# Larger sine slots, one exponential block for eight heads, and permuted rotary partners in an audio tower kernel

## The chip, the cores and the metric

The kernel runs on one core of a Trainium2 chip. A core has a matmul engine (PE in the profile), a vector engine (DVE), an activation engine (ACT), a general engine (POOL) and a queue engine that starts transfers (SP). Each works through its own list of instructions in order; semaphores hold an instruction until what it needs is there. The metric is the device time of one launch in microseconds (us).

## The reference

There are 32 sequences of audio. Each is cut into S = 313 frames of 512 samples, transformed (a cosine transform), and run through one layer: attention, then a feed-forward part in which every element goes through sines and cosines.

```python
h = einsum(frames, D)                              # 313 x 512 per sequence
h = h + attn(layernorm(h))                         # 8 heads of 64
h = h + ffn(layernorm(h))

# attention
Q = xpos(X @ W_Q, False); K = xpos(X @ W_K, True)  # x * cos + rot(x) * sin
p = softmax(Q @ K.T) * Dmat                        # decay gamma ** |n - m|
Y = groupnorm(p @ V)                               # over each head's 64
out = silu(X @ W_G) * Y @ W_O

# feed-forward, N = 256 units, D = 512 features
theta = x[..., None, :] / (1 + abs(W)) + B         # S x 256 x 512
idx = mod(round(theta * 4096 / (2 pi)), 4096)
cos_sum = sum(cos_tab[idx] * attn_cos, -1)         # over the 512 features
sin_sum = sum(sin_tab[idx] * attn_sin, -1)
out = silu(cos_sum @ proj_cos.T + sin_sum @ proj_sin.T)
```

The feed-forward part sets the size of the work: 32 x 313 x 256 x 512 angles, each with a sine and a cosine. With features on the 128 partitions that is 20.5 million elements per partition on ACT.

## The kernel before

**Feed-forward.** The 512 features are four chunks of 128 partitions (`c`), the 256 units are eight blocks of 32 (`UNITS`). Sequences are handled in pairs; pair p enters in round `STARTS[p]` and stays eight rounds, one for each block of units. So a round (`ffn_round`) works on one block for all pairs that are in: one to four pairs, that is r = 2, 4, 6 or 8 sequences. There are 42 rounds: 6 with r = 2, 8 with r = 4, 6 with r = 6 and 22 with r = 8. A *part* is one unit and one chunk for all r sequences. A *slot* takes as many parts as fit `SLOT` = 16 sequence-parts: 16 // r of them. In each slot

- DVE writes one index tile per part (`index`, L619), a second tile shifted by a quarter turn (`quarter`, L631), and wraps both (`mask`, L636), in int16;
- ACT takes two sines of the slot's tile (`sines`, L644: `trig<-ix`), one after the other, k = 1 and k = 0;
- PE sums over the features (`go`, L666): for each sequence and part a matmul with a 32 column weight (`hot`) that adds into row n of a PSUM bank (`pa`). Each is recorded as two instructions.

`ix` has three buffers of two halves, `trig` three, `hot` three. A `trig` buffer is free again when the matmuls of its slot have read it. The input `xT` of each pair stays in SBUF as long as the pair is in (`load_xT`, one load for each chunk). When a block is done DVE copies the bank (`part`, L684) and SP stores it in `sums_d`. After its eighth round, `output` loads the sums of a sequence (L531), projects them (four rows of `in_proj` through the two ring buffers), applies silu and adds the residual.

**Attention.** `attention` does one sequence: transform, layer norm, transposes, V, then for two halves of four heads: two times `columns` for q and k and, with weights whose neighbouring columns are swapped (`wq_s`, `wk_s`), for their rotary partners; multiplication by a table (`turn_qk`, L345) and addition (L349); for each head scores on PE (L359), the row maximum (L367) and a subtraction (L376) on DVE, but for each half's last head the maximum goes into ACT's bias. Then one ACT block `exps` per half: with `eng == "DVE"` one exponential over three heads (L383) and three over the last (L388), and a tiny Silu at the end (L396) that brings back the function table which the sines use. Then, head by head, transposes (L424), the decay (L436, from a tile `dec` loaded for each head) and the product with V (L442). Five sequences (the first two and three in the rounds with one pair) run with `eng == "ACT"`: there ACT does the evacuations and the exponentials of each head, with the row sums by accumulation; for the other 27 DVE does the sums.

**Order.** The kernel first collects all operations in a `Plan`: each has a key (its place in the intended order), an engine, an assumed duration and what it reads and writes. `emit` then plays them through: whichever engine is free next takes, of its operations that are ready, the one with the lowest key. The result is a fixed list for each engine. The first two sequences (buffers `A` and `B`) run before any sine and side by side; then `swap` gives B's space to the feed-forward part, and attention for the other 30 sequences, with buffers `A`, is spread over the rounds of sines so that each pair is ready in time.

Of the kernel before, what the change touches and what calls it, by code (L numbers as in the profile page):

```python
# [12 lines left out]
F32 = mybir.dt.float32  # L13
I32 = mybir.dt.int32
I16 = mybir.dt.int16
# [15 lines left out]
SLOT = 16  # L31
# [14 lines left out]
class Plan:  # L46
# [3 lines left out]
    WAIT = 400.0  # L50
    LAND = 3500.0
# [75 lines left out]
def tile_audio_tower(ctx: ExitStack, tc: tile.TileContext, t: dict, out: bass.AP):  # L127
# [6 lines left out]
    NB = 4  # L134
    N_RING = 2
    N_IX, N_TRIG, N_HOT, N_PA = 3, 3, 3, 4
# [10 lines left out]
    sums_d = dram.tile([2, P, 2, n_seq * S], F32, name="sums_d")  # L147
# [4 lines left out]
    class Buffers:  # L152


        def __init__(self, name, pool, psum):
# [3 lines left out]
            self.probs = [(name, "prob", a) for a in range(NB - 1)]  # L159
# [5 lines left out]
            self.dec = sb("dec", STEP * (NT - 1) + S)  # L165

            self.u = sb("u", NC4, S)
            self.qk = [self.u[:, 2 * i : 2 * i + 2, :] for i in range(2)]
# [3 lines left out]
            self.prob = sb("prob", NB - 1, NT, S)  # L172
            self.probT = sb("probT", NT, S)

            self.exp = [*(self.prob[:, a] for a in range(NB - 1)), self.probT]
            wide = self.prob.rearrange("p a b s -> p (a b s)")
            self.wide = wide
            self.turn = wide[:, NT * S : NT * S + 4 * S].rearrange("p (i s) -> p i s", s=S)
# [118 lines left out]
    def attention(plan, keys, sq, x, eng):  # L297
# [20 lines left out]
        hs, probs, us = x.rows_of, x.probs, x.every("u", 2)  # L318
# [14 lines left out]

        for hb in range(H // NB):
            for g in range(hb * NB // 2, (hb + 1) * NB // 2):
                key = step(4)
                qk = x.qk[g % 2]
                kq = x.k("u", g % 2)
                columns(plan, key, x, 0, t["wq"][g])
                columns(plan, key, x, 1, t["wk"][g])  # L340

                columns(plan, key, x, 2, t["wq_s"][g])
                columns(plan, key, x, 3, t["wk_s"][g])
                plan.add(key, "DVE", 1500,
                         lambda: nc.vector.tensor_tensor(  # L345
                             x.turn, x.W[:, :, :S], turn_qk, ALU.mult),
                         x.banks(0, 1, 2, 3), probs[1:])
                plan.add(key, "DVE", 870,
                         lambda qk=qk: nc.vector.tensor_tensor(  # L349
                             qk, x.turn[:, 0:2], x.turn[:, 2:4], ALU.add),  # L350
                         probs[1:], (kq,))
            for hd in range(hb * NB, (hb + 1) * NB):
                key = step(2.5)
                a, r0 = hd % NB, (hd % 2) * DH
                qk, kq = x.qk[hd // 2 % 2], x.k("u", hd // 2 % 2)
                for i in range(NT):
                    plan.add(
                        key, "PE", 660,
                        lambda i=i, qk=qk, r0=r0: nc.tensor.matmul(  # L359
                            x.W[:N, i, :S], qk[r0 : r0 + DH, 0, ROW0[i] : ROW0[i] + N],  # L360
                            qk[r0 : r0 + DH, 1, :], start=True, stop=True,
                        ),
                        (kq,), x.banks(i),
                    )
                m = x.mx[hd % 2]
                plan.add(key, "DVE", 1150,
                         lambda m=m: nc.vector.tensor_reduce(m[:N], x.W[:N, :NT, :S], AX.X, ALU.max),  # L367
                         x.banks(0, 1, 2), (x.k("mx", hd % 2),))
                if a == NB - 1:

                    plan.add(key, "DVE", 100,
                             lambda m=m: nc.vector.tensor_scalar(m[:N], m[:N], -1.0, None, ALU.mult),
                             (), (x.k("mx", hd % 2),))
                    continue
                plan.add(key, "DVE", 1150,
                         lambda m=m, a=a: nc.vector.tensor_tensor(  # L376
                             x.prob[:N, a], x.W[:N, :NT, :S],
                             m[:N].unsqueeze(2).to_broadcast((N, NT, S)), ALU.subtract),
                         (x.k("mx", hd % 2), *x.banks(0, 1, 2)), (probs[a],))

            def exps(hb=hb, m=m):
                if eng == "DVE":
                    nc.scalar.activation(x.prob[:N], x.prob[:N], AF.Exp)  # L383
                for a in range(NB):
                    for i in range(NT):
                        last = a == NB - 1
                        if last or eng == "ACT":
                            nc.scalar.activation(  # L388
                                x.exp[a][:N, i, :],
                                x.W[:N, i, :S] if last else x.exp[a][:N, i, :], AF.Exp,  # L390
                                bias=m[:N, i : i + 1] if last else 0.0,
                                accum_out=x.sm[:N, i, hb * NB + a : hb * NB + a + 1]
                                if eng == "ACT" else None,
                            )

                nc.scalar.activation(x.lu[:1, 0:1], x.lu[:1, 0:1], AF.Silu)  # L396
            plan.add(step(), "ACT", 10500 if eng == "ACT" else 6700, exps,
                     (x.k("mx", 1), *x.banks(0, 1, 2)),
                     [*probs, x.k("probT"), x.k("sm", hb), x.k("lu")])
            if eng == "DVE":  # L400
                h0 = hb * NB
                plan.add(step(0), "DVE", 1190,
                         lambda h0=h0 + NB - 1: nc.vector.tensor_reduce(
                             x.sm[:N, :, h0], x.probT[:N], AX.X, ALU.add),
                         (x.k("probT"),), (x.k("sm", hb),))
                plan.add(step(0), "DVE", 3160,
                         lambda h0=h0: nc.vector.tensor_reduce(
                             x.sm[:N, :, h0 : h0 + NB - 1].rearrange("p i h -> p h i"),
                             x.prob[:N], AX.X, ALU.add),
                         probs, (x.k("sm", hb),))  # L410

            for hd in (hb * NB + a for a in (3, 2, 0, 1)):
                key = step(5)
                a = hd % NB
                ka = (*probs, x.k("probT"))[a]
                plan.add(key, "SP", DMA_NS,
                         lambda hd=hd: nc.sync.dma_start(x.dec, t["decay"][hd]),
                         (), (x.k("dec"),))
                for jj in range(NT):
                    j = NT - 1 - jj  # L420

                    def go(a=a, jj=jj, j=j):
                        for i in range(NT):
                            nc.tensor.transpose(  # L424
                                x.W[:N, jj, ROW0[i] : ROW0[i] + N],
                                x.exp[a][:N, i, ROW0[j] : ROW0[j] + N], ident[:N, :N],
                            )
                    plan.add(key, "PE", 800, go, (ka,), x.banks(jj))

                def decayed():  # L430
                    window = x.dec[:N].rearrange("p (a s) -> p a s", a=1)
                    w3 = bass.AP(
                        tensor=window.tensor, offset=window.offset,
                        ap=[list(window.ap[0]), [STEP, NT], [1, S]],
                    )
                    nc.vector.tensor_tensor(x.probT[:N], x.W[:N, :NT, :S], w3, ALU.mult)  # L436
                plan.add(key, "DVE", 1150, decayed, (x.k("dec"), *x.banks(0, 1, 2)),
                         (x.k("probT"),))
                for i in range(NT):
                    def go(i=i, hd=hd):  # L440
                        for jj in range(NT):
                            nc.tensor.matmul(  # L442
                                x.y[:N, i, (hd % 2) * DH : (hd % 2 + 1) * DH],
                                x.probT[:N, jj, ROW0[i] : ROW0[i] + N],
                                x.h[:N, jj, hd * DH : (hd + 1) * DH],
                                start=(jj == 0), stop=(jj == NT - 1),
                            )
                    plan.add(key, "PE", 1000, go, (x.k("probT"), hs[hd // 2]), x.banks(3))
                if a not in (2, 1):
                    continue  # L450


                h0 = hd // 2 * 2
                plan.add(
                    step(), "DVE", 560,
                    lambda h0=h0: nc.vector.tensor_copy(  # L456
# [121 lines left out]
    def ffn_round(plan, k0, blk, ring):  # L578
# [22 lines left out]
        for parts in slots:  # L601
            first, last = parts is slots[0], parts is slots[-1]
            E = len(parts) * r * S
            for n, c in dict.fromkeys((n // 2 * 2, c // 2 * 2) for n, c in parts):
                if (n, c) in hot:
                    continue
# [351 lines left out]
```

## Time and profile before

| | |
|---|---|
| median of 3 runs | 18688.12 us (18686.35 to 18691.65) |
| the profiled execution | 18689.4 us |
| its span, first to last instruction | 18687.6 us |
| ACT busy | 18069.0 us, 97% |
| DVE busy | 17425.4 us, 93% |
| PE busy | 14667.1 us, 78% |
| sines (L644) | 4288 instructions, 17529.0 us of ACT |
| first sine | 353.6 us after the start |
| transfers | 783.70 MB, 42 GB/s mean |

The profile lists instruction groups by source line, engine and operation; behind the bar stands the idle time of the engine just ahead of them and what ended most of it. A long mean of an ACT or DVE row can overlap with its neighbour, so busy time divided by the count, or a run of equal instructions in the timeline, gives the price of one more.

### The profile page before, as it was taken

To read this page: it belongs to the slowest core of one execution; us is meant where nothing else is said; L and a number is where in the kernel's file an instruction comes from. 1 tells how busy PE (TensorE), PEld (TensorE's weight loads), DVE (VectorE), ACT (ScalarE), POOL (GpSimd) and SP (SyncE) were. 2 spreads that over 40 slices of the span, in tenths; PEclk is the share of its full clock that TensorE was granted. 3 is DMA by queue.
4 is the path that set the end of the run, shared out by engine and by line. 5 is a ranking of instruction groups with operands and counts; after the bars stand their busy time and mean duration, and the time that the engine had idled before them with its cause. 6 is when DMAs were issued, how large, how long until landed. Compare 5 with 4: busy or idle time off the path is not lost. (4 is left out here: it accounts for less than half of the span.)

```text
span 18687.6 us, 332496 instructions
## 1 busy us (share of the span) xinstructions
PE 14667.1 (78%) x148864; PEld 6569.4 (35%) x148864; DVE 17425.4 (93%) x12972; ACT 18069.0 (97%) x5026; POOL 944.3 (5%) x1222
## 2 busy tenths in 40 slices
PE   8788888888787887888787888887888887766566
PEld 5443333333333333333333333333333333222222
DVE  5899999999999999999999999999999999889998
ACT  3899999999999999999999999999999999999998
POOL 0001000000000000000000000000000000000000
PEclk8899999999999999999999999999999999889988
DMA  3211111111111111111111111111111111000011
GB/s 93 62 55 47 53 58 47 49 52 49 31 34 38 47 41 42 34 37 49 38 46 40 32 45 41 46 42 41 34 38 49 39 46 37 21 10 25 13 31 48
DMA packets 716483, 783.70 MB, mean 42 GB/s; under 512 B 72336, under 2 KB 470928, under 8 KB 715056
## 3 DMA queue, kind: packets, MB, share of 16 engines
q1 hardware_dynamic: 715056, 762.43, 13.7%
q8 instruction: 1169, 19.15, 0.4%
q14 instruction: 258, 2.11, 0.0%
HBM read 657.51 MB, written 104.66 MB: 41 GB/s over the span
## 5 line engine op out<-in xcount | busy, mean ns | idle before, releaser
L644 ACT ACTIVATE trig<-ix 128x5008 f32<-128x5008 int16 (+1 forms) x4288 | 17529.0, 4176 | 274.4 <-PE pa L666 157.3
L666 PE MATMUL pa<-trig,hot 128*32 128x313 f32 x131072 | 10264.9, 458 | 3322.3 <-ACT trig L644 3268.9
L666 PEld LDWEIGHTS pa<-trig,hot 128*32 128x32 f32 x131072 | 4033.6, 115 | 9141.6 <-ACT trig L644 4999.8
L619 DVE TENSOR_SCALAR ix<-xT,f 128x2504 int16<-128x2504 f32 (+3 forms) x5888 | 6658.2, 1182 | 49.3 <-DMA xT<-xT_d 31.3
L636 DVE TENSOR_SCALAR ix<-ix 128x10016 int16<-128x10016 int16 (+1 forms) x2144 | 5687.0, 2653 | 67.5
L631 DVE TENSOR_SCALAR ix<-ix 128x5008 int16<-128x5008 int16 (+1 forms) x2144 | 3029.4, 1413 | 622.0 <-ACT trig L644 485.3
L292 PE MATMUL a_W<-a_xnT,a_ring 128*128 128x313 f32 x4960 | 1514.5, 444 | 73.5 <-DVE a_prob L345 32.0
L277 PE MATMUL a_W<-a_ring,a_u 128*105 128x512 f32 x2256 | 1098.8, 619 | 84.7 <-DMA a_u<-in_frames 30.3
L292 PEld LDWEIGHTS a_W<-a_xnT,a_ring 128*128 128x128 f32 x4960 | 888.3, 190 | 693.8 <-issue 301.0
L442 PE MATMUL a_W<-a_h,a_probT 105*105 105x64 f32 x4464 | 540.7, 271 | 72.4 <-DVE a_probT L436 71.4
L277 PEld LDWEIGHTS a_W<-a_ring,a_u 128*105 128x105 f32 x2256 | 356.9, 174 | 683.0 <-issue 616.1
L442 PEld LDWEIGHTS a_W<-a_h,a_probT 105*105 105x105 f32 x4464 | 478.8, 182 | 326.4 <-issue 204.2
L228 POOL TENSOR_TENSOR a_gu<-a_gr 105x24 f32<-105x24 f32 x93 | 86.4, 929 | 9806.9 <-DVE a_gr L222 9802.1
L359 PE MATMUL a_W<-a_u 64*105 64x313 f32 x1488 | 485.3, 454 | 93.2 <-DVE a_prob L376 67.0
L277 PE MATMUL a_W<-a_ring,a_xnT 128*105 128x512 f32 x744 | 367.8, 618 | 30.0 <-DVE a_xnT L214 28.8
L359 PEld LDWEIGHTS a_W<-a_u 64*105 64x105 f32 x1488 | 232.7, 172 | 355.4 <-DVE a_prob L376 131.0
L228 POOL TENSOR_TENSOR a_lu<-a_lr 105x3 f32<-105x3 f32 x186 | 145.4, 782 | 3833.3 <-DVE a_lr L222 3823.5
L264 PE MATMUL a_W<-ident,a_h 105*128 105x105 f32 x1116 | 182.8, 293 | 158.0 <-DVE a_h L252 77.1
L367 DVE TENSOR_REDUCE a_mx<-a_W 105x3 f32<-105x939 f32 x248 | 279.8, 1128 | 20.0 <-PE a_W L359 19.8
L436 DVE TENSOR_TENSOR a_probT<-a_W,a_dec 105x939 f32<-105x939 f32 x248 | 279.7, 1128 | 19.3 <-PE a_W L424 17.1
L424 PE MATMUL a_W<-ident,a_prob 105*105 105x105 f32 x1674 | 243.2, 276 | 15.8 <-DVE a_h L456 15.8
L345 DVE TENSOR_TENSOR a_prob<-a_W,turn_qk 128x1252 f32<-128x1252 f32 x124 | 180.4, 1455 | 73.5 <-PE a_W L292 37.3
(138 smaller groups left out, 3748.7 us busy)
## 6 DMA issues: line engine op xcount, KB each, us to landing
hot<-in_hot SPq DMA_DIRECT2D x1344, 128.0 KB
a_dec<-in_decay SPq DMA_DIRECT2D x248, 260.5 KB
a_ring<-in_proj SPq DMA_DIRECT2D x128, 256.0 KB
a_ring<-in_dct SPq DMA_DIRECT2D x124, 256.0 KB
a_ring<-wv_d SPq DMA_DIRECT2D x124, 256.0 KB
a_ring<-in_wq SPq DMA_DIRECT2D x124, 256.0 KB
a_ring<-in_wk SPq DMA_DIRECT2D x124, 256.0 KB
a_ring<-in_wq_s SPq DMA_DIRECT2D x124, 256.0 KB
```

The lines of the kernel that those rows point to most:

```text
L277: lambda c=c, i=i, k=k, to=to: nc.tensor.matmul(x.W[:N, to, :], lhsT[:, c, ROW0[i] : ROW0[i] + N], x.ring[k], start=(c == 0), stop=(c == N ...
L292: lambda c=c: nc.tensor.matmul(x.W[:, bank, :S], w[:, c, :], x.xnT[:, c, :], start=(c == 0), stop=(c == NC4 - 1)),
L359: lambda i=i, qk=qk, r0=r0: nc.tensor.matmul(x.W[:N, i, :S], qk[r0 : r0 + DH, 0, ROW0[i] : ROW0[i] + N], qk[r0 : r0 + DH, 1, :], start=Tru ...
L367: lambda m=m: nc.vector.tensor_reduce(m[:N], x.W[:N, :NT, :S], AX.X, ALU.max),
L424: nc.tensor.transpose(x.W[:N, jj, ROW0[i] : ROW0[i] + N], x.exp[a][:N, i, ROW0[j] : ROW0[j] + N], ident[:N, :N],)
L436: nc.vector.tensor_tensor(x.probT[:N], x.W[:N, :NT, :S], w3, ALU.mult)
L442: nc.tensor.matmul(x.y[:N, i, (hd % 2) * DH : (hd % 2 + 1) * DH], x.probT[:N, jj, ROW0[i] : ROW0[i] + N], x.h[:N, jj, hd * DH : (hd + 1) * ...
L619: nc.vector.tensor_scalar(now["ix", x][:, 0, d0 : d0 + 2 * m * S], now["xT", c][:, 2 * at * S : 2 * (at + m) * S], f[:, 0, c, n : n + 1], ...
L631: nc.vector.tensor_scalar(tl[:, 1, :E], tl[:, 0, :E], float(LUT // 4), None, ALU.add)
L636: nc.vector.tensor_scalar(tl, tl, LUT - 1, LUT // 2, ALU.bitwise_and, ALU.bitwise_xor)
L644: nc.scalar.activation(tl[:, :E], now["ix", x][:, 1 - k, :E], AF.Sin, bias=-PI32, scale=ANG)
L666: nc.tensor.matmul(now["pa", p][g * 32 : g * 32 + 32, :S], now["hot", hot[n - u, c // 2 * 2]][:, u, c % 2, k, :], now["trig", w][:, s0 : s ...
```

## The change

Several edits come together.

1. `SLOT` goes from 16 to 24 sequence-parts. The `ix` buffers become five single halves in one tile, taken two at a time in turn, so that every fifth slot has halves that don't lie side by side and is wrapped by two `mask` instructions. `trig` goes from three buffers of 16 to two of 24, `hot` from three to four of the same bytes. Parts go chunk by chunk (all 32 units of a chunk, then the next), and `xT` and the scales `f` are loaded for each chunk of each round into two buffers, for all r sequences at once, so that one `index` instruction does a part.
2. `exps` stands once for all eight heads. `prob` grows from three heads to eight; every head subtracts its maximum on DVE; the decay writes back into `prob`; the decay tiles lie in the two halves of `u`; the table `turn_qk` is loaded for each sequence into `prob`'s space.
3. For the first two sequences `wq_s` and `wk_s` are not used: ACT copies q and k to SBUF, and a matmul with a permutation `swap_m` makes their partners.
4. `affine` and `centre` (one-time preparation of weights) get keys that place them after the start of the first sequences; `affine` no longer writes `h`.
5. `sums_d` is laid out by block: four sequences are stored by one transfer, and `output` loads eight pieces per sequence where it loaded two.
6. The scheduler's constants: `WAIT` 400 to 300, `LAND` 3500 to 2500, 150 ns for 169 per matmul of `go`.

```diff
-SLOT = 16
+SLOT = 24
...
-    WAIT = 400.0
-    LAND = 3500.0
+    WAIT = 300.0
+    LAND = 2500.0
...
-    N_IX, N_TRIG, N_HOT, N_PA = 3, 3, 3, 4
+    N_X, N_IX, N_TRIG, N_HOT, N_PA = 2, 5, 2, 4, 4
...
+            if swap_m is None:
                 columns(plan, key, x, 2, t["wq_s"][g])
                 columns(plan, key, x, 3, t["wk_s"][g])
+            else:
+                copy(plan, key, eng, 2 * S, x.raw, x.W[:, 0:2, :S], x.banks(0, 1), probs[-1:])
+                for i in range(2):
+                    plan.add(key, "PE", 550,
+                             lambda i=i: nc.tensor.matmul(x.W[:, 2 + i, :S], swap_m, x.raw[:, i, :],
+                                                          start=True, stop=True),
+                             probs[-1:], x.banks(2 + i))
...
+        def exps():
+            if eng == "DVE":
+                for a in range(0, H, 4):
+                    nc.scalar.activation(x.prob[:N, a : a + 4], x.prob[:N, a : a + 4], AF.Exp)
+            else:
+                for a in range(H):
                     for i in range(NT):
+                        nc.scalar.activation(x.prob[:N, a, i, :], x.prob[:N, a, i, :], AF.Exp,
+                                             accum_out=x.sm[:N, i, a : a + 1])
+
+            nc.scalar.activation(x.lu[:1, 0:1], x.lu[:1, 0:1], AF.Silu)
+        plan.add(step(2), "ACT", 18200 if eng == "ACT" else 9500, exps,
+                 (), [*probs, x.k("sm"), x.k("lu")])
+        if eng == "DVE":
+            for a in range(0, H, 2):
+                plan.add(step(0), "DVE", 2080,
+                         lambda a=a: nc.vector.tensor_reduce(
+                             x.sm[:N, :, a : a + 2].rearrange("p i h -> p h i"),
+                             x.prob[:N, a : a + 2], AX.X, ALU.add),
+                         probs[a : a + 2], (x.k("sm"),))
...
-        todo = [(n + u, c) for n in range(0, UNITS, 2) for c in range(NC4) for u in range(2)]
+        todo = [(n, c) for c in range(NC4) for n in range(UNITS)]
...
+            for c in dict.fromkeys(c for n, c in parts):
+                if c not in xs:
+                    y, fz = xs[c], fs[c] = place("xT", N_X), place("f", N_X)
...
+                    plan.add(key - 10, "SP", DMA_NS,
+                             lambda c=c, y=y: nc.sync.dma_start(
+                                 new("xT", y, [P, RING * S], bufs=N_X)[:, : r * S],
+                                 xT_d[:, c, sq0 * S : (sq0 + r) * S]),
+                             [("xT_d", sq0 + b) for b in range(r)], (("xT", y),))
...
-            x = place("ix", N_IX)
+            x = [place("ix", N_IX) for _ in range(2)]
...
+                for i in ([slice(x[0], x[1] + 1)] if x[0] < x[1] else [slice(i, i + 1) for i in x]):
+                    nc.vector.tensor_scalar(ix[:, i, :E], ix[:, i, :E], LUT - 1, LUT // 2,
+                                            ALU.bitwise_and, ALU.bitwise_xor)
...
-    affine(plan, -2000.0, A)
+    affine(plan, -999.9, A)
...
-    centre(plan, -1999.0, B)
+    centre(plan, -999.93, B)
```

## The prediction

> **What bounds the kernel now.** I read the engines' shares first, then the busy time by stretch of the span, then ACT's groups by shape and ACT's waits.
>
> ```profile
> PE 14667.1 (78%) x148864; PEld 6569.4 (35%) x148864; DVE 17425.4 (93%) x12972; ACT 18069.0 (97%) x5026; POOL 944.3 (5%) x1222
> ```
>
> ACT is busy for all but 618.6 us of the span. The stretches say where those lie (columns: length, busy PE, weight loads, DVE, ACT, POOL, clock, DMA share, GB/s):
>
> ```profile
> 200.00:300.00 100.00, 92.33 (x385) 68.03 (x384) 46.07 (x56) 22.64 (x58) 7.32 (x26) 0.71 0.22 66
> ...
> 400.00:1000.00 600.00, 484.97 (x4286) 252.50 (x4278) 541.50 (x664) 494.31 (x222) 34.46 (x52) 0.89 0.21 62
> ...
> 5000.00:15000.00 10000.00, 8080.53 (x82744) 3594.39 (x82748) 9502.80 (x6123) 9995.33 (x2559) 554.13 (x684) 0.95 0.14 41
> ```
>
> There are three regimes. Until the first sine (353.6 us) PE carries the first two sequences. From there to about 1000 us ACT, DVE and PE are all near full and wait for each other. From 5000 to 15000 us ACT has no gap (99.95%), while DVE has 5% and PE 19%. So after the ramp an ACT microsecond saved is a microsecond of time, as long as nothing new makes ACT wait. What ACT is made of:
>
> ```profile
> L644 ACT ACTIVATE trig<-ix 128x5008 f32<-128x5008 int16 x3520 | 15046.3, 4363 | 218.2 <-PE pa L666 138.6 <-DVE ix L636 53.6 <-DVE a_u L349 13.7
> L644 ACT ACTIVATE trig<-ix 128x3756 f32<-128x3756 int16 x768 | 2483.0, 3319 | 56.2 <-issue 19.2 <-PE pa L666 18.7 <-DVE ix L636 14.9
> L383 ACT ACTIVATE a_prob<-a_prob 105x2817 f32<-105x2817 f32 x54 | 138.0, 2555 | 0.6
> ...
> ACT trig L644 <- PE pa L666: 157.3, 78, 7.1
> ACT trig L644 <- DVE ix L636: 68.5, 46, 10.4
> ```
>
> The last two rows are waits (total, times, longest). By stretch, the 157.3 us for PE fall as 78 in 400 to 1000 us, 59 in 1000 to 4000, about 6 in 4000 to 16000 and 14 at the end.
>
> **What the Trainium skill says.** "ScalarE: Activation LUTs", section What ACT_TABLE_LOAD costs: one element per cycle at 0.833 ns, 186 ns for an instruction with immediate operands, of which back-to-back ones hide 93; a table load is 1283 ns, and a drain of about 1380 ns makes a switch about 2.66 us. The trace agrees on slope, overlap and the 1283 ns, but shows no drain: the next instruction begins within 0.02 us of the load's end. "Perfetto Trace Analysis", section Optimization Strategy: repeated gaps on an engine that should be full can mean too few buffers. That is the thing to fear of `trig` going from three to two.
>
> **The change, part by part.**
>
> *Sines.* Built, the changed program's order has 2688 sines of 7512 elements, 56 of 5008 and 16 of 2504: 2760 for 4288, with the same 20.5 million elements. So 1528 instructions' fixed time goes. Runs of equal sines price it:
>
> ```profile
> 8154.05 158.00 ACT L644 ACTIVATE trig<-ix 128x5008 f32<-128x5008 int16 x37
> ...
> 17298.24 503.06 ACT L644 ACTIVATE trig<-ix 128x3756 f32<-128x3756 int16 x156
> ```
>
> That is 4.270 and 3.225 us each, 0.835 ns per element and 88 ns fixed; with the skill's 0.833 ns the fixed part is 98. 1528 x 88 to 98 = 134 to 150; I take **-145**. All of it is on the bound.
>
> *Exponentials.* A half now takes 6.50 us of ACT from load to Silu (8147.55 to 8154.05 in the timeline): two loads of 1.28, 2.55, three of 0.44, 0.20. The new block is two loads, two instructions of 3756 (2.555 + 939 x 0.833 ns = 3.34 each, 0.1 overlapped) and 0.2: 9.28. 27 sequences x (13.00 - 9.28) = **-100**. Of the five ACT sequences, three run beside sines and save a pair of loads and a Silu, 2.8 each: **-8**. This rests on no Exp being left between sines, which the order shows.
>
> *Start.* For the first two sequences 64 matmuls of 128x313 go (2.28 us per four at the timeline's clock, 36 us) and 16 of that size come (9 us), PE being 92% busy there. The ACT copy between (626 elements; 1252 take 1.19 us, so some 0.65) is covered: three or four matmuls of the other sequence stand in PE's order between. Two more subtractions of 1.14 us for each sequence (5 us) lie on DVE, about full while scores run. Moving `affine` and `centre` behind the first loads lets PE start before 16.1 us, where it now waits for `in_dct` behind 2.7 MB of other loads; the same 14 us of DVE come later, beside PE's transform. But the first slot takes DVE 12.7 instead of 8.4 us. -27 + 5 - 4 + 4 = **-22** on the first sine's time; from -45 to +10, since one block of 48 exponentials for both sequences (0.45 each, 21 us) now stands where two shorter ones were, and PE may wait for B's.
>
> *Waits of ACT for PE.* Not shown by the trace, so bounded. A group of matmuls takes PE 2.31 us for 16 (a run of 32 instructions at full clock; 2.47 by busy time over count), so 3.5 to 3.7 for 24. With three buffers of 16 PE could be 6.0 us late before ACT stopped; with two of 24 it is 6.36 - 3.7 - 0.1 = 2.6 us. Attention's matmuls stand between the groups in PE's order. I charged each its time (0.58 to 0.62 us for 128x313, 0.88 to 0.97 for 512 columns, 0.20 to 0.24 for PV), took off what a period leaves free (2.65 us, now 1.8), carried the rest on, and called what exceeds the slack a wait. For the order before this gives 87 to 203 us, and 157 were measured; for the order after 155 to 356. The larger groups are 6 matmuls of 512 (5.3 us) and 8 of 313 (4.6 us) in one go, where PE used to take 2 or 3. Scaled: +50 in the ramp to 1000 us, +40 to 4000, +35 to 15000, -5 at the end, of which some falls into time in which DVE holds ACT anyway: **+100**, from 0 (attention stands still for transfers just where it would pile up) to +200.
>
> *DVE.* Index instructions fall from 5888 to 5376 (208 ns fixed, from 626 at 541 and 2504 at 1539 ns: -106), quarters by 764 (156 ns: -119), masks by 488 (173 ns: -84); 64 more subtractions at 1.136 (+73), 64 fewer sign changes (-11), row sums even. -247 in 17425: DVE keeps its distance to ACT. Five halves let it run 1 to 2 slots (13 to 25 us) ahead, where two slots were 17 us. I take **-20** off the 68.5 us, 0 at worst.
>
> *SP and transfers.* `xT` and `f` are 168 loads each for 64 and 42; `xT` adds 144 MB (8 GB/s on 42). They are keyed 10 half-slots (64 us) ahead and a buffer lasts a quarter of a round (35 us at r = 2, 136 at r = 8). The queue gets 4138 entries for 4049; the decay loads stop holding it (2180 us waiting for L436 with one buffer). The table load per sequence waits for heads 4 and 5 of the sequence before; only the first rotary step needs it. I cost these at nothing, hidden under running sines; if the cover is gone, each late chunk stalls DVE, then ACT. At the end one slot is shorter and six more small loads per sequence (0.6 us each) stand before the last projection: **+4**.
>
> Sum: -145 - 100 - 8 - 22 + 100 - 20 + 4 = -191 on the profiled 18689.4 (span 18687.6), giving 18498; the median is 1.3 us below that. I take 18490.
>
> **The rivals.**
> *The cover holds* (0.27): the late matmuls cost nothing new, ACT idles as before. -145 - 100 - 8 - 22 - 20 + 4: 18398. For it: the measured waits from 5000 to 15000 us are 1.6 us, where the count gave up to 27. Against: in the ramp the count comes out near the waits.
> *Two sine buffers make PE the pacemaker* (0.09): 722 of the groups have more than 2.65 us of attention ahead of them in PE's order. If each costs ACT 0.7 us, because attention also waits for DVE in mid-burst with the sine matmuls queued behind, it is 505 us on the 18398 of the case above: 18903. It is slower than before from 0.4 us per group (290 gained over 722). Against: it needs such waits in the middle stretch, where today there are none.
> *Late chunks* (0.10): 1 us for each of 168 chunk changes, PE's +100 on top: 18660. For: `xT` reloads are new in every round, up to 1.28 MB each. Against: the DMA share is 14%.
> That the change doesn't do what it says is excluded for the counts (they are in the built order); not for the start.
>
> **How the numbers follow.** The main case (0.48) is 18490, between 18400 and 18590 by the bounds of the start and of PE's waits. The rest, 0.06, is small mishaps around no change. About 0.2%, 37 us, is what a measurement of this kernel can tell from no change. Faster by more: main, cover and most of late chunks, 0.86; within: 0.05; slower: 0.09. Range 18350 to 18660.
>
> **What would show it.** After the change ACT's group of sines should be 2760 strong with about 17384 us; ACT busy about 17816, idle about 681; one pair of table loads per sequence; the first sine near 330 us. The row of sines waiting for PE should be about 250 us; near 157 is the second case, above 500 the third. DVE waiting for `xT` above 100 us is the fourth. I am wrong if ACT's busy time falls by much other than 255 us, or if its idle time leaves 550 to 750 us.

## The result, and the profile after

The kernel after takes 18588.61 us (median of five runs, 18575.13 to 18593.15), the kernel before 18688.12 us on the same chip (five runs, 18683.11 to 18698.63). The ratio is 0.9944, 95% interval 0.9931 to 0.9957: about 105 us less, from 80 to 129 (the medians differ by 99.5). The forecast was 18490 with a range of 18350 to 18660. The direction and the range held; the gain is about half of what was predicted. The profiled execution of the kernel after took 18593.15 us, with a span of 18591.2 us, 96.4 less than before.

The shares of the engines, as the page of the kernel after has them:

```profile
PE 14520.5 (78%) x148768; PEld 6791.6 (37%) x148768; DVE 17165.7 (92%) x11210; ACT 17827.2 (96%) x3248; POOL 968.9 (5%) x1222
```

ACT's busy time fell by 241.8 us (18069.0 to 17827.2), and DVE's by 259.7. But the span fell by only 96.4, so ACT's idle time rose by 145.4 (618.6 to 764.0). ACT's groups show the first half of this (first all sines, then groups by shape), and the rows of waits (who waits for whom: total, times, longest) show the second, with two rows of the kernel before at the end:

```profile
L636 ACT ACTIVATE trig<-ix 128x7512 f32<-128x7512 int16 (+1 forms) x2760 | 17398.1, 6386 | 456.8 <-PE pa L658 229.7
...
L636 ACT ACTIVATE trig<-ix 128x7512 f32<-128x7512 int16 x2688 | 17122.8, 6453 | 423.8 <-PE pa L658 200.9 <-DVE ix L628 128.1 <-issue 80.0
...
L400 ACT ACTIVATE a_prob<-a_prob 105x3756 f32<-105x3756 f32 x54 | 177.1, 3327 | 0.3
...
L407 ACT ACT_TABLE_LOAD x32 | 41.1, 1283 | 0.6
...
L400 ACT ACT_TABLE_LOAD x27 | 34.6, 1283 | 0.5
```

```profile
ACT trig L636 <- PE pa L658: 229.7, 132, 8.8
...
ACT trig L636 <- DVE ix L628: 128.1, 56, 13.4
...
ACT trig L636 <- issue: 81.3, 21, 7.4
...
PE a_W L282 <- DMA a_u<-in_frames: 52.9, 21, 6.5
```

```profile
ACT trig L644 <- issue: 27.9, 11, 5.8
...
PE a_W L277 <- DMA a_u<-in_frames: 30.3, 9, 7.2
```

There are 2760 sines in all with 17398.1 us, against 4288 with 17529.0. One pair of table loads is left for each of the 27 sequences with `eng == "DVE"`. The three waits of the sines, for PE, for DVE and for nothing the profile names ("issue"), were 157.3, 68.5 and 27.9 us before. They are now 72, 60 and 53 longer. One stretch of the span shows most plainly that something new is there (length, busy PE, weight loads, DVE, ACT, POOL, clock, DMA share, GB/s):

```profile
5000.00:15000.00 10000.00, 7971.06 (x82855) 3728.56 (x82857) 9439.75 (x5534) 9883.89 (x1657) 592.60 (x671) 0.93 0.16 50
```

From 5000 to 15000 us ACT had no gap before (9995.33 busy); now 116 us are missing there, though DVE (94%) and PE (80%) are both less loaded than before. So no engine has become too full on the average of this stretch; some work seems to come at the wrong moment.

The first sine now comes 316.2 us after the start (353.6 before):

```profile
316.18 25.53 ACT L636 ACTIVATE trig<-ix 128x7512 f32<-128x7512 int16 x4 [10.47 <-DVE ix L628]
```

The span can be made up from these numbers. ACT's busy time gives -241.8 us. Its idle time until the first sine fell from 300.7 to 264.8, that is -35.9. After the first sine it rose from 317.9 to 499.2, that is +181.3. Together this is -96.4.

**One case of an "issue" wait.** The timeline of the kernel after (start, length, engine, line, count, and in brackets the wait ahead of it), cut to PE, ACT and SP's queue:

```profile
9011.59 0.34 SPq L596 DMA_DIRECT2D xT<-xT_d  x1
9011.98 0.42 SPq L326 DMA_DIRECT2D a_u<-in_frames  x1
...
9018.60 5.71 PE L282 MATMUL a_W<-a_ring,a_u 128*105 128x512 f32 x8 [4.82 <-DMA a_u<-in_frames]
...
9024.24 3.37 PE L658 MATMUL pa<-trig,hot 128*32 128x313 f32 x48
...
9027.73 12.82 ACT L636 ACTIVATE trig<-ix 128x7512 f32<-128x7512 int16 x2 [4.66 <-issue]
```

The load of the frames (`in_frames`, 626 KB) goes out 0.4 us behind a chunk of `xT` of 1252 KB. PE has reached the transform of the next sequence (L282), stands for 4.8 us and starts 6.6 us after the load was issued. The sine group at 9024.24 is queued behind it, ends at 9027.6, and only then is a `trig` buffer free: the sine starts at 9027.73. The wait is called "issue", but what it goes back to is a transfer two steps earlier.

The place in the queue matters. From 6700 to 15300 us the kernel after issues 16 loads of frames, and the timeline shows PE waiting for 14 of them. Seven of the 14 were issued 0.4 us behind a chunk of `xT`, and PE started 6.5 to 7.2 us after their issue; it waited 30.5 us for these in all. The other seven had no chunk just ahead, and PE started 3.8 to 4.7 us after their issue; it waited 3.7 us for these.

**One case of a wait for PE**, from the timeline at 5123 us (PE and ACT, and one copy on DVE):

```profile
5123.41 5.40 PE L282 MATMUL a_W<-a_ring,a_xnT 128*105 128x512 f32 x12
5128.73 3.37 PE L658 MATMUL pa<-trig,hot 128*32 128x313 f32 x48
5132.03 5.40 PE L282 MATMUL a_W<-a_ring,a_xnT 128*105 128x512 f32 x12
...
5138.64 0.48 DVE L675 COPY part<-pa 128x313 f32<-128x313 f32 x1
...
5140.03 6.53 PE L658 MATMUL pa<-trig,hot 128*32 128x313 f32 x96 [2.60 <-ACT trig L636]
5143.51 12.82 ACT L636 ACTIVATE trig<-ix 128x7512 f32<-128x7512 int16 x2 [3.54 <-PE pa L658]
```

Two lumps of six matmuls with 512 columns (5.40 us each, two recorded instructions for one matmul) stand close together in PE's order, and ACT's next sine waits 3.54 us. Lumps of this kind are what the prediction counted, but here they explain only a part. PE is through with the second lump at 5137.43, yet its next sine group starts at 5140.03, and the profile puts these 2.60 us down to ACT. Had the group (3.37 us) started at once, the sine would have waited about 0.9 us by estimate. The stand falls at the turn of a round: by the code, this group is the first of the new round in two PSUM banks that the round before had filled, and DVE's last copy of them (`part`, L675) ran from 5138.64 to 5139.12. The kernel after also has one `part` buffer where the kernel before has two. Whether that is the cause, and what it is worth elsewhere, was not tested.

### The profile page after: what moved, and what is told of

Same layout as the page of the kernel before. It is cut to its first block, busy times and chain, and to the rows that moved or that the text cites. A ratio compares the mean times of both kernels' runs of the same rounds, so it can differ in the third digit from the quotient of the medians.

```text
span 18591.2 us, 325962 instructions
## 1 busy us (share of the span) xinstructions
PE 14520.5 (78%) x148768; PEld 6791.6 (37%) x148768; DVE 17165.7 (92%) x11210; ACT 17827.2 (96%) x3248; POOL 968.9 (5%) x1222
## 5 line engine op out<-in xcount | busy, mean ns | idle before, releaser
L636 ACT ACTIVATE trig<-ix 128x7512 f32<-128x7512 int16 (+1 forms) x2760 | 17398.1, 6386 | 456.8 <-PE pa L658 229.7
L658 PEld LDWEIGHTS pa<-trig,hot 128*32 128x32 f32 x131072 | 4291.2, 118 | 9312.4 <-ACT trig L636 4578.4
L612 DVE TENSOR_SCALAR ix<-xT,f 128x2504 int16<-128x2504 f32 (+3 forms) x5376 | 6499.2, 1268 | 431.6 <-ACT trig L636 389.4
L628 DVE TENSOR_SCALAR ix<-ix 128x15024 int16<-128x15024 int16 (+4 forms) x1656 | 5581.8, 3385 | 41.1
L621 DVE TENSOR_SCALAR ix<-ix 128x7512 int16<-128x7512 int16 (+1 forms) x1380 | 2905.2, 2105 | 356.1 <-ACT trig L636 264.4
L282 PE MATMUL a_W<-a_ring,a_u 128*105 128x512 f32 x2256 | 1087.5, 625 | 141.2 <-DMA a_u<-in_frames 52.9
L282 PEld LDWEIGHTS a_W<-a_ring,a_u 128*105 128x105 f32 x2256 | 374.7, 177 | 756.3 <-issue 615.0
L446 PE MATMUL a_W<-a_h,a_prob 105*105 105x64 f32 x4464 | 483.0, 264 | 77.6 <-DVE a_prob L440 77.4
L446 PEld LDWEIGHTS a_W<-a_h,a_prob 105*105 105x105 f32 x4464 | 447.3, 177 | 212.1 <-issue 143.7
L282 PE MATMUL a_W<-a_ring,a_xnT 128*105 128x512 f32 x744 | 350.6, 611 | 22.3 <-DVE a_xnT L219 20.5
L428 PEld LDWEIGHTS a_W<-ident,a_prob 105*105 105x105 f32 x2232 | 237.9, 178 | 159.4 <-issue 92.5
L440 DVE TENSOR_TENSOR a_prob<-a_W,a_u 105x939 f32<-105x939 f32 x248 | 279.8, 1128 | 16.3 <-PE a_W L428 10.9
L385 DVE TENSOR_TENSOR a_prob<-a_W,a_mx 105x939 f32<-105x939 f32 x248 | 281.7, 1136 | 8.5
```

What stands on the lines that cost most here:

```text
L282: lambda c=c, i=i, k=k, to=to: nc.tensor.matmul(x.W[:N, to, :], lhsT[:, c, ROW0[i] : ROW0[i] + N], x.ring[k], start=(c == 0), stop=(c == N ...
L385: lambda: nc.vector.tensor_tensor(x.prob[:N, hd], x.W[:N, :NT, :S], m[:N].unsqueeze(2).to_broadcast((N, NT, S)), ALU.subtract),
L428: nc.tensor.transpose(x.W[:N, jj, ROW0[i] : ROW0[i] + N], x.prob[:N, a, i, ROW0[j] : ROW0[j] + N], ident[:N, :N],)
L446: nc.tensor.matmul(x.y[:N, i, (hd % 2) * DH : (hd % 2 + 1) * DH], x.prob[:N, a, jj, ROW0[i] : ROW0[i] + N], x.h[:N, jj, hd * DH : (hd + 1) ...
L612: nc.vector.tensor_scalar(ix[:, x[0], pt * r * S : (pt + 1) * r * S], now["xT", y][:, : r * S], f[:, 0, n : n + 1], f[:, 1, n : n + 1], AL ...
L621: nc.vector.tensor_scalar(ix[:, x[1], :E], ix[:, x[0], :E], float(LUT // 4), None, ALU.add)
```

## The experiments

All times are medians, and ratios are to the kernel before on the same chip. The runs were spread over several chips, on which the kernel before took 18688.12 to 18692.73 us, so a difference of medians can be off by some 5 us besides the runs' own spread. The waits are those of one profiled execution for each kernel.

| kernel | time, us | ratio, 95% interval | sines wait for PE / DVE / issue, us |
|---|---|---|---|
| before | 18688.12 | 1 | 157 / 69 / 28 |
| after | 18588.61 | 0.9944, 0.9931 to 0.9957 | 230 / 128 / 81 |
| e1: slot of 16, three `trig` | 18697.60 | 1.0003, 0.9994 to 1.0011 | 117 / 268 / 27 |
| e2: slot of 16, two `trig` | 18933.04 | 1.0129, 1.0116 to 1.0143 | 357 / 133 / 78 |
| e3: frames assumed later | 18535.59 | 0.9916, 0.9902 to 0.9929 | 226 / 93 / 50 |
| e4: attention's matmuls spread | 18602.84 | 0.9951, 0.9938 to 0.9963 | 168 / 162 / 102 |
| e5: swapped weights back | 18613.41 | 0.9958, 0.9944 to 0.9971 | 220 / 134 / 80 |
| e6: preparation first | 18594.76 | 0.9946, 0.9933 to 0.9960 | 235 / 127 / 81 |
| e7: all three constants back | 18821.43 | 1.0067, 1.0054 to 1.0081 | 336 / 213 / 99 |
| e8: e3 and e4 | 18531.96 | 0.9913, 0.9900 to 0.9927 | 189 / 126 / 49 |
| e9: e3 and a lighter DVE in the ramp | 18531.99 | 0.9916, 0.9901 to 0.9930 | 210 / 48 / 63 |
| e10: before with the new constants | 18680.73 | 0.9994, 0.9985 to 1.0003 | 115 / 128 / 6 |
| e11: 169 ns back | 18643.16 | 0.9973, 0.9963 to 0.9983 | 330 / 61 / 105 |
| e12: WAIT and LAND back | 18723.33 | 1.0018, 1.0011 to 1.0026 | 240 / 216 / 56 |

### The slot undone (e1), and two buffers of 16 (e2)

e1 is the kernel after with the old slot and as much buffer space as it had; e2 takes one `trig` buffer from e1.

```diff
-SLOT = 24
+SLOT = 16
-    N_X, N_IX, N_TRIG, N_HOT, N_PA = 2, 5, 2, 4, 4
+    N_X, N_IX, N_TRIG, N_HOT, N_PA = 2, 6, 3, 4, 4     # e1
+    N_X, N_IX, N_TRIG, N_HOT, N_PA = 2, 6, 2, 4, 4     # e2
```

> The changed kernel with slots of 16 again, six index halves and three sine buffers; all other edits stay. Two theories. Buffers: the time that the prediction missed lies in ACT's new waits, since two sine buffers of 24 leave PE 2.6 us of slack where three of 16 left 6.0, and both attention's lumps of matmuls and late loads now reach ACT. Then the 131 us of sine overhead come back (sines 17529 us), but ACT's waits for PE fall from 230 to about 150, and the 81 us in which ACT waits for nothing that the profile shows fall below 30: about 18590, no difference to the changed kernel. Other edits: the waits come from the eight-head block, the chunk loads and the ramp, and stay: 18590 + 131 = 18720.

> The same with two sine buffers of 16 where it had three; it leaves PE 1.7 us of slack. Buffers theory: attention's matmuls charged between the sine groups of this order exceed the slack by 318 us where the changed kernel's do by 206 and the one with three buffers by 116; so ACT's waits for PE rise to some 350 us, and the time to about 18790. Other edits: no difference to three buffers.

e1 took 18697.60 us: without the slot, all the other edits together gain nothing, although ACT's list is 103 us shorter than before just the same (busy 17966.2). Of the two theories, the first had 18590 and the second 18720. The waits for PE and "issue" fell about as the first said, but neither had named the wait for DVE, which took the gain back:

```profile
ACT trig L636 <- DVE ix L628: 267.7, 146, 7.2
ACT trig L636 <- PE pa L658: 116.5, 60, 9.7
ACT trig L636 <- issue: 27.0, 13, 3.6
```

The wait for DVE is four times that of before (68.5). DVE is busy 17406.5 of a span of 18704.9 here, as in the kernel before, so a shorter ACT with an unchanged DVE is the likely reason. That isn't shown alone: the new order of chunks and the new constants are in e1 too, and on the kernel before the constants by themselves raise this wait from 69 to 128 (e10). No run takes back the eight-head block, the loads of `xT` by chunk or the layout of `sums_d` alone. The slot of 24 takes 241 us off DVE as well as 139 off ACT, and the sines' wait for DVE is 140 shorter with it than in e1. So the slot is worth 109 us (18697.60 less 18588.61) although it lengthens the waits for PE by 113 and "issue" by 54. The 140 are a gain of the slot that the prediction priced far too low: it had -145 for the sines, +100 for PE and only -20 for DVE.

e2 took 18933.04 us. Two buffers of 16 cost 235 us over three; two of 24 are 344 us better than two of 16. The sines' wait for PE is 357 us, as expected (350), but the time is 143 more than the 18790 expected. Of the 344 us, 160 are ACT's shorter list and 127 the wait for PE (the rest lies in other waits of ACT), so the larger slot pays for the third buffer in two ways: fewer instructions, and more time in which PE may be late.

### The late frames (e3)

The scheduler is told that a load of the frames takes 4.5 us longer. Nothing of the work changes; the order puts the transform later behind its load.

```diff
             end = t + dur + (self.LAND if e == "SP" else 0.0)
+            if e == "SP" and not ops[i][4] and len(ops[i][5]) == 2 and ops[i][5][0][1] == "u":
+                end += 4500.0
```

> The changed kernel, but its scheduler assumes 4.5 us more for the loads into u that depend on nothing (the frames of the next sequence), so that PE gets the matmuls that need them later in its order. Buffers theory: PE stood up to 6.5 us at these matmuls with the sine groups queued behind, because the frames queue behind a 1.25 MB chunk of xT; ACT's unexplained 81 us fall below 30 and PE's 53 us of waiting for in_frames below 20: 18535. Other edits: these gaps have another cause and stay, 18590 within 20.

It took 18535.59 us, 53 less than the kernel after, as expected. The waits of e3 (its lines stand two lower down):

```profile
ACT trig L638 <- PE pa L660: 226.4, 134, 8.3
...
ACT trig L638 <- DVE ix L630: 92.5, 49, 13.4
ACT trig L638 <- issue: 49.6, 18, 7.3
...
PE a_W L284 <- DMA a_u<-in_frames: 10.8, 11, 4.2
```

PE's wait for the frames fell from 52.9 to 10.8, "issue" by 32 and the wait for DVE by 36; the wait for PE stayed. From 4000 to 14600 us the three waits of the sines sum to 87 us for 137. So the late frames are a cause of the new gaps, and of "issue" above all. Late frames alone don't make the wait: in e1, with three `trig` buffers, PE waits 47.3 us for the frames and "issue" is only 27.0; in e2, with two buffers of 16, the two are 40.0 and 78.3. They seem to reach ACT where the buffers leave PE little slack. That DVE's wait fell too was part of the gain but isn't explained by the frames alone; the order of everything behind them changes with it, and only this one changed order was run.

### Spreading attention's matmuls (e4, e8)

The row, column and output matmuls get keys 0.6 of a sine apart, chunk by chunk, so that lumps like that at 5123 us are broken up. e8 does it on top of e3.

```diff
     def rows(plan, key, x, lhsT, src, r, order=range(NT), src_r=()):
+        gap = 0.6 if key > 0 else 0.0
...
-                    key, "PE", 880,
+                    key + gap * c, "PE", 880,
...
-            columns(plan, key, x, 1, t["wk"][g])
+            columns(plan, key + gap, x, 1, t["wk"][g])
...
-            columns(plan, key, x, g, t["wg"][g])
+            columns(plan, key + (0.6 * g if key > 0 else 0.0), x, g, t["wg"][g])
```

> The changed kernel with the keys of attention's and the output's matmuls spread: each chunk of a row product and each of the four column products is due 0.6 of a sine later than the one ahead, after the first two sequences. Buffers theory: charged the same way the order exceeds PE's slack by 5 us from 4000 to 15000 us where the changed kernel's does by 52, and by 134 for 143 in the ramp; ACT's waits for PE fall from 230 to about 150, and the time to 18520. Other edits: waits for PE are not from lumps, 18590 within 20.

> The later landing of the frames (18535 alone) and the spread keys (18603 alone) together. The spread alone took 62 us off ACT's waits for PE but put 25 us more on PE's wait for in_frames, 34 on ACT's for DVE and 20 on the unexplained ones. Buffers theory: with the frames out of the way the 62 us are kept; waits for PE about 165 us, unexplained 45: 18480. Rival: what the spread takes from PE's lumps returns as waits for DVE, which is near full to 4000 us; waits for DVE about 150 us: 18540.

In e4 the wait for PE fell from 230 to 168 us, as it was meant to, but the time didn't (18602.84, 18520 expected): the wait for DVE rose to 162 and "issue" to 102, and PE's wait for the frames to 78. In e8 the frames' part is gone ("issue" 49), and the same exchange is seen again: 37 us less for PE, 34 more for DVE, and 18531.96 us, no different from e3. So the lumps are a cause of the wait for PE, but in both runs what was taken from it came back as a wait for DVE. That attention, spread out, hands its results to DVE too late is the likely reason; it wasn't shown.

### The start (e5, e6)

e5 gives the first two sequences their matmuls with swapped weights again; e6 puts the preparation of weights first again.

```diff
-        attention(plan, lambda x: -1000.0 + x, b, (A, B)[b], "ACT", swap_m)     # e5
+        attention(plan, lambda x: -1000.0 + x, b, (A, B)[b], "ACT")
...
-    affine(plan, -999.9, A)                                                      # e6
+    affine(plan, -2000.0, A)
-    centre(plan, -999.93, B)
+    centre(plan, -1999.0, B)
```

> The changed kernel with wq_s and wk_s loaded and multiplied for the first two sequences too, no permutation matmul. The first sine came at 316.2 us for 353.6 before. Theory: most of these 37 us are the 48 matmuls of 128x313 that went (27 us); here the first sine comes at about 340 us and the end moves by as much, 18610. Rival: the start gains from affine and centre being moved and from the one exponential block; first sine within 8 us of 316, time within 15 us of 18590.

> The changed kernel with affine and centre keyed ahead of everything again (affine still does not write h). Theory of the matmuls: this is worth some 8 us of start, first sine at 324 us, 18597. Rival: the move is most of the 37 us, first sine at 340, 18610.

In e5 the first sine came at 345.5 us for 316.2 and the end 25 us later; in e6 at 325.6 and 6 us later. These make up the 37 us by which the start got shorter (353.6 to 316.2): some 29 from the permutation and some 9 from the keys. In e5, 29 us at the first sine are 25 at the end. e6's 6 us are within the spread of the runs; its first sine is what shows the effect.

### The scheduler's constants (e7, e10, e11, e12)

`WAIT` is the delay that the scheduler assumes before another engine sees a result, `LAND` the time that it assumes for a transfer to land, and the third number its time for one matmul of `go`. The prediction gave this edit no price. The assumed fixed part of a sine went from 110 to 100 ns as well; no run moves that one. e7 puts all three constants back, e11 and e12 parts of them, and e10 gives the new ones to the kernel before.

```diff
-    WAIT = 300.0
-    LAND = 2500.0
+    WAIT = 400.0                                       # e7, e12
+    LAND = 3500.0
...
-                plan.add(key, "PE", 150 * len(parts) * r, go,
+                plan.add(key, "PE", 169 * len(parts) * r, go,      # e7, e11
```

> The changed kernel with the scheduler's constants of before (WAIT 400, LAND 3500, 169 ns per sine matmul). Theory of late loads: a landing assumed 1 us later takes part of the waits for in_frames away (PE's 53 us to about 30, ACT's unexplained 81 to about 55), but more of attention's matmuls stand in lumps (225 us above the slack by the count for 206): 18580. Rival: the constants carry the gain, because DVE and PE are ordered too loosely with the old ones: 18640.

> The kernel before with the three scheduler constants of the kernel after (WAIT 300, LAND 2500, 150 ns for a matmul of go). Theory: the constants are worth time only where the order is short of slack, as with two sine buffers of 24; with three of 16 the kernel before keeps its 18688, 18660 to 18720, and ACT waits for PE about 160 us. Rival: the constants are a better model of the chip for any slot and carry the gain by themselves: 18590, ACT waiting for PE below 100 us.

> The kernel after with 169 ns again for each matmul of go in the scheduler; WAIT 300 and LAND 2500 stay. Theory: that price is most of what putting back all three constants cost (233 us): with it the sine groups look 12% longer to the scheduler, PE seems to be late and attention is dealt out in lumps; 18780, ACT waiting for PE near 310 us. Rival: the two latencies carry it: 18600, waits as in the kernel after.

> The kernel after with WAIT 400 and LAND 3500 again; 150 ns stays. Theory: the price of go's matmuls carries most of the 233 us, so this one costs little, 18620. Rival: the assumed latencies carry it: 18790, with more waits of ACT for DVE as well as for PE.

e7 took 18821.43 us, 233 more than the kernel after and more than the kernel before: neither side had expected it. On the kernel before the same three numbers do nothing that this measurement can tell (e10: 18680.73, interval 0.9985 to 1.0003), though they shift waits: of PE from 157 to 115, of DVE from 69 to 128. So the constants aren't better by themselves: they pay only together with other edits. That these are the slot and the buffers is likely but not shown, since the old constants with the slot of 16 and the other edits weren't run.

Of the 233 us, the price of the matmuls alone gives 55 (e11) and the two latencies 135 (e12); both together cost 43 more than the sum. The expectation that the price carries most of it fell; the latencies carry more, if less than the rival said. The rows of the sines' waits from 4000 to 14600 us, first of the kernel after, then of e11, then of e12:

```profile
ACT trig L636 <- PE pa L658: 69.6, 45, 8.8
...
ACT trig L636 <- DVE ix L628: 17.4, 11, 3.2
```

```profile
ACT trig L636 <- PE pa L658: 110.3, 60, 6.6
...
ACT trig L636 <- DVE ix L628: 2.5, 2, 1.7
```

```profile
ACT trig L636 <- DVE ix L628: 110.0, 77, 3.7
ACT trig L636 <- PE pa L658: 101.5, 58, 5.5
```

The two act mainly on different waits. With 169 ns the sines wait longer for PE (330 us in all for 230). With the longer latencies they wait longer for DVE (216 for 128), and all of that comes in the middle stretch, where DVE is no busier (10013.36 us in the kernel after, 9923.32 in e12, of 10600); there the wait for PE is 32 longer too, though not over the whole run. The first sine comes at 330.2 us for 316.2. What exactly in the order does it wasn't taken apart: WAIT and LAND were moved together only.

### A lighter DVE in the ramp (e9)

On top of e3, the sequences that attention does while two pairs are in use ACT for evacuations, exponentials and row sums, as those in rounds with one pair do.

```diff
-        narrow = len(rings[int(np.searchsorted(key_of, k, "right")) - 1]) <= 1
+        narrow = len(rings[int(np.searchsorted(key_of, k, "right")) - 1]) <= 2
```

> The kernel with the late-frames edit (18535 measured), and besides in the rounds with two pairs attention leaves its evacuations, exponentials and row sums to ACT, as so far only in the rounds with one pair. Theory: from 1000 to some 2500 us DVE is the bound and ACT waits for it; moving about 16 us of DVE work per sequence to ACT, which takes some 14 us for it, for four to six sequences, takes 10 to 30 us off: 18515, ACT waiting for DVE below 70 us. Rival: ACT and DVE are equally full there and ACT's extra 60 to 80 us lie on the bound later: 18560 or more.

It took 18531.99 us, 4 less than e3 and no different by the runs. From 1000 to 4000 us, first e3, then e9:

```profile
1000.00:4000.00 3000.00, 2444.02 (x24520) 1189.96 (x24516) 2887.18 (x2187) 2849.43 (x538) 194.49 (x254) 0.93 0.20 59
```

```profile
1000.00:4000.00 3000.00, 2442.74 (x24484) 1198.10 (x24488) 2837.42 (x2157) 2889.81 (x741) 195.37 (x254) 0.92 0.20 59
```

DVE lost 50 us there, and ACT gained 40. The sines' wait for DVE fell from 92.5 to 47.9 over the whole run, so DVE held ACT up in part of the ramp, as the theory has it. But ACT's own list is 39.5 us longer (17867.8 for 17828.3), and that eats most of it: one bound exchanged for another of nearly the same price.

The fastest versions are e3, e8 and e9, 18532 to 18536 us, which the runs don't tell apart. e3 is the smallest of them.

## Why the prediction was right, and half off in size

The forecast sum was -191 us, and the profiled span moved by -96.4. Of the 95 us between them, the wait for DVE is +80, the "issue" wait +53 and the sines +14; the wait for PE, the start, the exponentials and what is left give back 28, 14, 3 and 8. The prediction's own sign of being wrong, an idle time of ACT outside 550 to 750 us, came true with 764.0.

**Sines: right.** -130.9 us were measured for -145, or 86 ns for each of the 1528 instructions that went. The 88 ns that the runs of equal sines gave were nearer than the 98 that follow from the slope in the Trainium skill ("ScalarE: Activation LUTs", What ACT_TABLE_LOAD costs).

**Exponentials and table loads: right.** ACT's busy time fell by 110.9 beyond the sines, where 108 were counted. The new instruction of 3756 elements takes 3.327 us (3.34 expected), and the pairs of table loads went as counted.

**Start: right in sign, undersized.** -37 us on the first sine for -22. It lies within the range of -45 to +10. e5 and e6 split it as the prediction had it: permutation first, keys second; 29 and 9 us against 27 and 4. The terms that were to cost something (+5 and +4) didn't show.

**Waits for PE: right in the sum, wrong in the place.** 230 us were measured for "about 250"; the term was +100 and came out at +72. e4 shows that lumps of attention's matmuls cause part of it. But the prediction laid +50 before 1000 us, +40 up to 4000 and +35 after that. Measured were -10 up to 1000 us (78 before, 69 after), +9 from 1000 to 4000 and +65 from 4000 to 14600 (5 before, 70 after). So the count of slack rightly foresaw a wait in the middle stretch that no row yet showed, at about half its size, and foresaw one in the ramp that didn't come; that the sum is near is partly luck. The Trainium skill's advice ("Perfetto Trace Analysis", Optimization Strategy) that gaps may mean too few buffers fits e2, where one `trig` buffer less costs 235 us.

**DVE: the step that failed.** The term was -20, since DVE's busy time would fall by 247 (259.7 measured). The wait rose by 60 instead. By stretch, 40 of the 60 lie from 1000 to 4000 us (44.2 before, 84.5 after). The rows of that stretch, before and after:

```profile
1000.00:4000.00 3000.00, 2451.35 (x24324) 1152.36 (x24328) 2889.74 (x2440) 2881.99 (x880) 211.79 (x253) 0.94 0.17 50
...
ACT trig L644 <- DVE ix L636: 44.2, 34, 3.1
```

```profile
1000.00:4000.00 3000.00, 2448.07 (x24462) 1189.85 (x24458) 2887.30 (x2187) 2842.88 (x536) 197.59 (x254) 0.93 0.19 59
...
ACT trig L636 <- DVE ix L628: 84.5, 34, 13.4
```

DVE is as busy there as before (2889.7 and 2887.3 of 3000). Its index, quarter and mask instructions, which shrink by 330 us over the run, shrink by 23 there (2448 to 2426), and the rest of its work grows by 20; most of the saving lies after 5000 us, where DVE had time to spare. A sum over the whole run was set against a wait that belongs to one stretch. For about the same number of sine elements ACT is 39 us less busy there, so ACT meets DVE more often; e9 shows it by lifting DVE (62.3 us of this wait in e3, 26.0 in e9). One wait of 13.4 us, near 1017 us, is of another kind: the second pair's `xT`, which goes out to `xT_d` only at 995.38, arrives late. It is the only place after the first sine where DVE waits for `xT`.

**SP and transfers, costed at nothing: the other step that failed.** What was looked at was whether `xT` itself would be late. It rarely is (DVE waits 34.9 us for it, 31.3 before). What is late is another load that stands behind a chunk of it in the queue, and the one that waits is PE, with the sine groups in its order behind. The "issue" wait grew by 53; letting the order expect the delay takes 32 of them back, and the time falls by 53 (e3). One more step failed here without a visible price: the loads of the decay tiles were to stop holding the queue, but SP still waits 1655 us for L440 (2181 for L436 before).

**The constants had no price.** They decide 233 us (e7), more than any part that was costed. The direction rests on them: with the old constants the kernel after is 0.7% slower than the kernel before. The prediction read the built order, in which they were already at work, so its count of slack had them in for PE; but it could not say that the gain depends on them. In so far the right direction is luck.

**Slot and exponentials aren't additive.** In e1, 103 us less on ACT's list bring nothing, with DVE as long as it was. The prediction's "an ACT microsecond saved is a microsecond of time, as long as nothing new makes ACT wait" rests on its second half: without the slot, what ACT saves comes back as waits for DVE. The prediction had noted that DVE keeps its distance, but set only 20 us for it.

Of the rivals, "the cover holds" asked for a row near 157 us: 230 exclude it. Two buffers as pacemaker asked for over 500: excluded too, though 357 in e2 and 336 in e7 show how near the edge is. Late chunks asked for over 100 us of DVE waiting for `xT`: 34.9 exclude it in this form. Its chunks do harm, but by the frames behind them.

## What to carry to other kernels

When the engine that sets the time gets less to do, look at the next engine in the same stretch: compare the savings of both stretch by stretch, not as sums over the run. Where a list scheduler makes the order, its assumed durations are part of the kernel: after a change of slots or buffers they are worth measuring again, and a price of zero for such an edit isn't safe (here 233 us). When a small transfer starts to share a queue with new large ones, look for whoever waits for the small one, and for what is queued behind that.

## What was not expected of the hardware

A 626 KB load that is issued 0.4 us behind one of 1252 KB keeps PE waiting until 6.5 to 7.2 us after its issue, where 3.8 to 4.7 are seen with no such load just ahead, though the DMA engines' mean share is low (16% from 5000 to 15000 us). And the mean clock granted to PE fell from 0.934 to 0.918 between the two kernels without PE being busier; no run here shows whether that costs anything.
